# Rows of x for 12 of layer 0's 391 edge groups from one-hot products instead of gathers, in a two-layer graph network on one core

## The chip, the cores and the metric

The kernel runs on one core of a Trainium2 chip. The metric is the device time of one execution in microseconds (us). Three runs of the kernel before gave 4848.2 us as their median (4844.53 to 4863.56).

## The reference

There are 12,500 nodes with 48 features each and 200,000 edges, sorted by their destination. Cut to what matters:

```python
# layer 0
tmp = concat([x[dst], x[src], edge_attr_32], axis=1)      # 48 + 48 + 32 = 128 columns
msg = relu(tmp @ W1 + b1) @ W2 + b2
x1  = layernorm(x + segment_sum(msg, dst))
# layer 1
m   = relu(x1[src] + edge_attr_48)
out = layernorm(x1 + (1 + eps) * x1 + segment_sum(m, dst))
```

Because the edges are sorted by dst, a run of neighbouring edges touches only a short window of destination nodes. The sources are random, so x[src] and x1[src] need a row from anywhere in the table.

## The kernel before

The edges are cut into 391 groups of 512, each four tiles of 128 edges, one edge on each partition. The nodes are padded to 98 blocks of 128 rows; 14 segments of 7 blocks (896 rows) are finished one after the other.

**Rows of the sources.** GpSimd (POOL) issues one indirect DMA for each tile (`gather`, line 201), four a group, from x in layer 0 (`fetch0`, line 399) and from x1 in DRAM in layer 1 (`fetch1`). Each gather reads 128 rows of 192 bytes.

**Layer 0, group g.** The tile cat holds, for each edge, a one-hot of its destination in a window of 48 nodes, the gathered row, and the edge's 32 features. `fill0` (line 404) writes the features (ACT) and the one-hot (VectorE, line 302), and loads the window's rows of x @ W1a, computed beforehand by `project`, to the first 48 rows of the weights wcat (SP's queue, line 412). `turn0` transposes cat on TensorE into pt (line 417) and VectorE copies it to cat_t (line 419). `hidden0` multiplies it by wcat into ph (line 424), and ACT applies the bias and the relu. `message0` multiplies by W2 into pm (line 432), and VectorE adds b2. `sum0` multiplies the one-hots by the messages into pa (line 323), and VectorE adds pa to the segment's sums at a register offset (line 318).

**Layer 1, group g.** VectorE adds the gathered rows and the edge features (line 495), ACT applies the relu (line 497), and TensorE sums over the destinations as before (line 323).

**Products instead of gathers in layer 1.** For 28 of the 391 groups, every 13th from 26, nothing is gathered. `finish0` splits each finished segment of x1 into three bf16 pieces, whose sum is x1, and keeps them in SBUF (xp: 98 blocks, 3 pieces, 48 columns). `split_src` splits each source index into its row within a block and its block. `place` makes, for two groups at a time, a one-hot of the row times the block's number plus one, and transposes it. For each block b, `select` (line 525) compares this with b + 1 on VectorE, which leaves a one-hot in bf16 for those edges whose source lies in block b, and `multiply` (line 530) multiplies it by the block's three pieces and accumulates in PSUM. After all 98 blocks the three pieces are added (line 570).

**Order.** The order of every engine's work is that of the program (`manual_schedule`); semaphores are set from the tiles used. `run` walks in steps k and calls the stages with an offset: in layer 0, in step k, POOL fetches group k + 5, fill0 works on k + 2, sum0 on k - 3, message0 on k - 2, hidden0 on k - 1 and turn0 on k. Then comes `lead0` (line 457), which loads and projects segments in due steps. In layer 1 `lead1` calls `next(work1)` in each step, so the products go on by one batch of four blocks (BPS) a step: 32 products for two groups of four tiles. A generator that has done its 25 batches closes its pair of groups in one more step. There are ten cat buffers, so POOL can run ahead of TensorE by several groups. `finish0` comes in the stage of sum0, for the segment whose last group that is.

Of the kernel before, what the change touches and what calls it, by code (L numbers as in the profile page):

```python
# [24 lines left out]
F32 = mybir.dt.float32  # L25
I32 = mybir.dt.int32
BF16 = mybir.dt.bfloat16
AF = mybir.ActivationFunctionType
ALU = mybir.AluOpType
AX = mybir.AxisListType  # L30

P = 128
Q = 128
N = 12500
E = 200000
D = 48
# [4 lines left out]
NT = -(-N // Q)  # L41
NPAD = NT * Q
TPC = 4
CHUNK = P * TPC
NCHUNK = -(-E // CHUNK)
EPAD = NCHUNK * CHUNK

W = 48
R = 80
NB = 7  # L50
NSEG = NT // NB
# [4 lines left out]
AHEAD = 5  # L56
NW = 4
EC = 5
FIRST = 26
EVERY = 13  # L60
NPE = 28
BATCH = 2
PIECES = 3
BPS = 4

PE_GROUPS = [FIRST + EVERY * i for i in range(NPE)]
assert PE_GROUPS[-1] < NCHUNK and NPE % BATCH == 0

assert NSEG * NB == NT
STEP = CHUNK * N // E  # L70
# [58 lines left out]
def windowed(ctx, tc, dram, flag, x, src, dst, e32, e48, w1, b1, w2, b2, eps, out):  # L129
    nc = tc.nc  # L130
    const = ctx.enter_context(tc.tile_pool(name="const", bufs=1))
    onehots = ctx.enter_context(tc.tile_pool(name="onehots", bufs=2 * BPS))
    cats = ctx.enter_context(tc.tile_pool(name="cats", bufs=AHEAD + 5))
    echunk = ctx.enter_context(tc.tile_pool(name="echunk", bufs=3))
    work = ctx.enter_context(tc.tile_pool(name="work", bufs=2))
    aggs = ctx.enter_context(tc.tile_pool(name="aggs", bufs=3))
    node = ctx.enter_context(tc.tile_pool(name="node", bufs=2))
# [104 lines left out]
        nc.vector.tensor_copy(flag, pf)  # L242


    part = const.tile([P, NPE, TPC], F32, name="part")
    block = const.tile([P, NPE, TPC], F32, name="block")

    def split_src():
        first = FIRST * TPC
        some = src_i[:, first : first + (NPE - 1) * EVERY * TPC].rearrange(  # L250
            "p (i c) -> p i c", c=EVERY * TPC
        )[:, :, 0:TPC]
        last = src_i[:, PE_GROUPS[-1] * TPC : (PE_GROUPS[-1] + 1) * TPC]
        bits = node.tile([P, NPE, TPC], I32, name="bits")
        for op, by, plus, to in (
            (ALU.bitwise_and, Q - 1, 0.0, part), (ALU.logical_shift_right, 7, 1.0, block)
        ):
            nc.vector.tensor_scalar(bits[:, : NPE - 1, :], some, by, None, op0=op)
            nc.vector.tensor_scalar(bits[:, NPE - 1, :], last, by, None, op0=op)
            nc.vector.tensor_scalar(to, bits, plus, None, op0=ALU.add)  # L260


    def project(s):
# [37 lines left out]
    def one_hot(o, g):  # L301
        nc.vector.tensor_tensor(
            o, iota_w[:, None, :].to_broadcast([P, TPC, W]),
            rel[:, g, :, None].to_broadcast([P, TPC, W]), op=ALU.is_equal,
        )
# [53 lines left out]
    def rows_of(table, s):  # L359
        return table[s * SN : (s + 1) * SN, :].rearrange("(t p) d -> p t d", p=Q)  # L360

    def finish0(s):
        pn = segment_sums(0, s)
        y = node.tile([Q, NB, D], F32, name="y")
        nc.vector.tensor_tensor(y, pn, x_seg.pop(s), op=ALU.add)
        x1 = node.tile([Q, NB, D], F32, name="x1")
        layer_norm(x1, y)
        nc.sync.dma_start(rows_of(x1_dram, s), x1)
        for i in range(PIECES):
            piece = xp[:, s * NB : (s + 1) * NB, i, :]  # L370
            nc.scalar.activation(piece, x1, AF.Copy)
            if i < PIECES - 1:
                rest = node.tile([Q, NB, D], F32, name="rest")
                nc.vector.tensor_tensor(rest, x1, piece, op=ALU.subtract)
                x1 = rest

    def finish1(s):
        pn = segment_sums(1, s)
# [9 lines left out]
    def last_group(s):  # L388

        return max(g for g in range(NCHUNK) if low(g) < (s + 1) * SN)  # L390
# [3 lines left out]
        finishes.setdefault(last_group(s), []).append(s)  # L394


    cat, ph, h, pm, hot = {}, {}, {}, {}, {}

    def fetch0(g):
        cat[g] = cats.tile([P, TPC, Q], F32, name="cat")  # L400
        for j in range(TPC):
            gather(cat[g][:, j, W : W + D], x, g, j)

    def fill0(g):
        e = load_edges("e32c", e32, DE, g)
        nc.scalar.activation(cat[g][:, :, W + D :], e, AF.Copy)
        one_hot(cat[g][:, :, :W], g)
        s = seg_of(g)
        at = nc.sync.value_load(
            off[0:1, g : g + 1], min_val=low(g) - seg_start(s), max_val=high(g) - seg_start(s)  # L410
        )
        nc.sync.dma_start(wcats[g % NW][0:W, :], a_dram[s][bass.ds(at, W), :])

    def turn0(g):
        pt = psum.tile([Q, TPC, P], F32, name="pt", bufs=2)
        for j in range(TPC):
            nc.tensor.transpose(pt[:, j, :], cat[g][:, j, :], ident[:P, :P])  # L417
        cat_t = work.tile([Q, TPC, P], F32, name="cat_t")
        nc.vector.tensor_copy(cat_t, pt)  # L419
        h[g] = cat_t  # L420
# [36 lines left out]
    def lead0(k):  # L457
        for s in range(1, NSEG):
            if k == first_group(s - 1) + 4:
                load_seg(x, s)  # L460
            if k == first_group(s - 1) + 8:
                project(s)
        if k == 14:
            check_windows()
        if k == 16:
            split_src()

    for g in range(AHEAD):
        fetch0(g)
    project(0)  # L470
# [4 lines left out]
    )  # L475


    made = {}

    def fetch1(g):  # L480
        if g in PE_GROUPS:
            return
        cat[g] = cats.tile([P, TPC, D], F32, name="xs")
        for j in range(TPC):
            gather(cat[g][:, j, :], x1_dram, g, j)
# [5 lines left out]

    def message1(g):
        m = work.tile([P, TPC, D], F32, name="m")
        xs = made.pop(g) if g in PE_GROUPS else cat.pop(g)
        nc.vector.tensor_tensor(m, xs, h[g], op=ALU.add)  # L495
        msg = work.tile([P, TPC, D], F32, name="msg1")
        nc.scalar.activation(msg, m, AF.Relu)  # L497
        h[g] = msg
# [2 lines left out]
        pa = reduce_tiles(hot.pop(g), h.pop(g))  # L501
        add_window(1, g, pa)


    tiles = BATCH * TPC
    PER = 512 // (PIECES * D)
    SUMS = ("ph", "pm", "pt")

    def place(first):

        which = psum.tile([Q, tiles, P], BF16, name="pt", bufs=2)
        for i in range(BATCH):
            which_e = work.tile([P, TPC, Q], BF16, name="which_e")
            for j in range(TPC):
                nc.vector.tensor_scalar(
                    which_e[:, j, :], iota_q, part[:, first + i, j : j + 1],
                    block[:, first + i, j : j + 1], op0=ALU.is_equal, op1=ALU.mult,
                )
            for j in range(TPC):
                nc.tensor.transpose(which[:, i * TPC + j, :], which_e[:, j, :], ident16)  # L520
        return which

    def select(which, b):
        o = onehots.tile([Q, tiles, P], BF16, name="o")
        nc.vector.tensor_scalar(o, which, float(b + 1), None, op0=ALU.is_equal)  # L525
        return o

    def multiply(ps, o, b):
        for k in range(tiles):
            nc.tensor.matmul(  # L530
                ps[k // PER][:, k % PER, :], o[:, k, :], xp[:, b, :, :],
                start=False, stop=False, skip_group_check=True,
            )

    def edge_of(ps, start):
        for t in ps:
            n = t.shape[1] * PIECES * D
            nc.tensor.matmul(
                t.rearrange("p k c d -> p (k c d)"), zeros[:, :P], zeros[:, :n],
                start=start, stop=not start,  # L540
            )

    zeros = const.tile([1, 512], BF16, name="zeros")
    nc.vector.memset(zeros, 0.0)

    def products():

        for first in range(0, NPE, BATCH):
            due = PE_GROUPS[first]
            which = place(first)  # L550
            ps = [
                psum.tile([P, min(PER, tiles - k * PER), PIECES, D], F32, name=name,
                          bufs=2 if name == "pt" else 1)
                for k, name in enumerate(SUMS)
            ]
            edge_of(ps, True)
            last = []
            for b in range(0, NT, BPS):
                now = [(b + i, select(which, b + i)) for i in range(min(BPS, NT - b))]
                for c, o in last:  # L560
                    multiply(ps, o, c)
                last = now
                yield due
            for c, o in last:
                multiply(ps, o, c)
            edge_of(ps, False)
            xs = work.tile([P, tiles, D], F32, name="made")
            for k, t in enumerate(ps):
                n = t.shape[1]
                nc.vector.tensor_reduce(  # L570
                    xs[:, k * PER : k * PER + n, :], t.rearrange("p k c d -> p k d c"),
                    AX.X, ALU.add,
                )
            for i in range(BATCH):
                made[PE_GROUPS[first + i]] = xs[:, i * TPC : (i + 1) * TPC, :]
            yield due

    work1 = products()

    def lead1(k):  # L580
        next(work1, None)
# [216 lines left out]
```

## Time and profile before

| | us |
|---|---|
| median of the runs | 4848.2 (4844.53 to 4863.56) |
| the profiled execution's own time | 3846.41 |
| its span | 3844.6 |
| busy: POOL | 2887.0 (75%) |
| busy: TensorE (PE) | 2856.8 (74%) |
| busy: VectorE (DVE) | 1893.4 (49%) |
| busy: ACT | 564.0 (15%) |
| mean granted TensorE clock | 0.787 |

The profile is one execution, and it is 1002 us shorter than the median of the runs; its rows are durations in that execution. The page gives busy time by engine, then 40 equal slices of the span (the granted TensorE clock, PEclk, in tenths), then the costliest groups of instructions: line, engine, operation, tiles, count, busy time, mean ns of one, and the idle time of the engine just before them with what ended it ("issue" is idle time that ends for no reason that the profile shows). PEld is TensorE's weight load, which overlaps its products. Layer 0 lasts until about 1970 us, layer 1 from there to the end.

### The profile page before, as it was taken

The page shows a single profiled execution, that of the slowest core. Times are in us where ns is not written, and L with a number is a line of the kernel's source. Part 1 is how long each engine was busy: PE and PEld are TensorE (multiplying, and loading weights), DVE is VectorE, ACT ScalarE, POOL GpSimd, SP SyncE. Part 2 cuts the span into 40 slices and gives each one's busy share as a digit, 9 for nine tenths or more (in the row PEclk, how much of TensorE's full clock was granted, in tenths as well). Part 3 has the DMA queues.
Part 4 walks back from the last instruction along what each step waited for, and adds up shares of the span by engine and source line. Part 5 has one row for each costly group of instructions (what it writes and reads, how often), then busy time and mean ns, then how long its engine had stood idle before and what let it go on. Part 6 is the DMA issues. An engine that isn't in the chain of part 4 may idle for free. (4 is left out here: it accounts for less than half of the span.)

```text
span 3844.6 us, 67581 instructions
## 1 busy us (share of the span) xinstructions
PE 2856.8 (74%) x23396; PEld 2210.8 (58%) x23396; DVE 1893.4 (49%) x4618; ACT 564.0 (15%) x1329; POOL 2887.0 (75%) x3025
## 2 busy tenths in 40 slices
PE   6888788888888888888886767667677676667731
PEld 4555555556555555556565656656566666656631
DVE  3333333333333333333356766767677676767731
ACT  2222212212212212212110000000000000000000
POOL 7777777777777777777767777777777777777776
PEclk9787877787777777777778888878887887888765
DMA  3222222222222222222222221222122222212221
GB/s 71 43 45 49 44 44 47 46 40 49 49 39 49 45 41 47 48 41 46 38 44 39 50 39 37 55 45 43 38 50 43 45 43 50 43 33 55 45 42 28
DMA packets 293005, 171.68 MB, mean 45 GB/s; under 512 B 109664, under 2 KB 292400, under 8 KB 292656
## 3 DMA queue, kind: packets, MB, share of 16 engines
q0 software_dynamic: 96512, 74.31, 13.1%
q1 hardware_dynamic: 179248, 84.31, 8.0%
q10 hardware_dynamic: 16896, 8.69, 0.7%
q8 instruction: 185, 3.03, 0.3%
q14 instruction: 164, 1.34, 0.1%
HBM read 154.45 MB, written 12.62 MB: 43 GB/s over the span
## 5 line engine op out<-in xcount | busy, mean ns | idle before, releaser
L201 POOL DMA_INDIRECT cat<-in_x_dram,src_i x1564 | 1485.1, 950 | 481.0 <-issue 339.5
L201 POOL DMA_INDIRECT xs<-x_dram,src_i x1452 | 1400.0, 964 | 461.0 <-issue 340.7
L530 PEld LDWEIGHTS <-o 128*128 128x128 bf16 x10976 | 853.0, 112 | 22.6 <-DVE o L525 0.6
L525 DVE TENSOR_SCALAR o<-pt 128x1024 bf16<-128x1024 bf16 x1372 | 848.7, 677 | 5.4 <-PE pt L520 5.4
L419 DVE COPY cat_t<-pt 128x512 f32<-128x512 f32 x391 | 270.2, 691 | 897.5 <-PE pt L417 897.5
L323 PE MATMUL pa<-hot,msg 128*48 128x48 f32 x3128 | 255.8, 234 | 561.3 <-ACT msg L497 561.2
L417 PEld LDWEIGHTS pt<-ident,cat 128*128 128x128 f32 x1564 | 265.6, 176 | 632.2 <-DMA cat<-in_x_dram,src_i 365.1
L424 PE MATMUL ph<-cat_t,wcat 128*128 128x512 f32 x782 | 580.3, 833 | 0.8 <-DVE cat_t L419 0.8
L323 PEld LDWEIGHTS pa<-hot,msg 128*48 128x48 f32 x3128 | 202.6, 144 | 642.3 <-ACT msg L497 623.1
L530 PE MATMUL ph<-xp,o 128*128 128x144 bf16 x4116 | 568.5, 256 | 0.0
L417 PE MATMUL pt<-ident,cat 128*128 128x128 f32 x1564 | 389.4, 347 | 237.2 <-DMA cat<-in_x_dram,src_i 233.9
L530 PE MATMUL pm<-xp,o 128*128 128x144 bf16 x4116 | 563.9, 254 | 0.0
L432 PE MATMUL pm<-w_sb,h 128*128 128x48 f32 x3128 | 538.0, 326 | 1.3 <-ACT h L426 1.2
L432 PEld LDWEIGHTS pm<-w_sb,h 128*128 128x128 f32 x3128 | 484.0, 236 | 27.8 <-ACT h L426 2.4
L426 ACT ACTIVATE h<-ph,b_sb 128x512 f32<-128x512 f32 x391 | 268.4, 686 | 1370.1 <-PE ph L424 1355.6
L530 PE MATMUL pt<-xp,o 128*128 128x144 bf16 x2744 | 453.8, 253 | 0.0
L495 DVE TENSOR_TENSOR m<-xs,e48c 128x192 f32<-128x192 f32 x363 | 131.4, 362 | 549.6 <-DMA xs<-x_dram,src_i 549.0
L497 ACT ACTIVATE msg<-m 128x192 f32<-128x192 f32 x391 | 141.8, 363 | 1611.9 <-DVE m L495 1611.9
L323 PE MATMUL pa<-cat,msg 128*48 128x48 f32 x3128 | 260.8, 237 | 33.4 <-DVE msg L434 25.6
L323 PEld LDWEIGHTS pa<-cat,msg 128*48 128x48 f32 x3128 | 207.8, 147 | 112.1 <-issue 52.9
L434 DVE TENSOR_TENSOR msg<-pm,b_sb 128x192 f32<-128x192 f32 x391 | 139.5, 357 | 233.6 <-PE pm L432 231.3
L318 DVE TENSOR_TENSOR agg<-agg,pa 48x48 f32 x782 | 150.3, 192 | 174.0 <-PE pa L323 122.9
(79 smaller groups left out, 1066.8 us busy)
## 6 DMA issues: line engine op xcount, KB each, us to landing
e48c<-in_e_dram SPq DMA_DIRECT2D x78, 480.0 KB
cat<-in_x_dram,src_i POOLq DMA_INDIRECT x1564
e32c<-in_e_dram SPq DMA_DIRECT2D x78, 320.0 KB
xs<-x_dram,src_i POOLq DMA_INDIRECT x1452
wcat<-a SPq DMA_DIRECT2D x391, 24.0 KB
a<-a ACTq DMA_DIRECT2D x14, 256.0 KB
a<-a ACTq DMA_DIRECT2D x14, 192.0 KB
x_seg<-in_x_dram SPq DMA_DIRECT2D x14, 168.0 KB
```

The source lines that it names most:

```text
L201: nc.gpsimd.indirect_dma_start(out=t, out_offset=None, in_=table, in_offset=bass.IndirectOffsetOnAxis(ap=src_i[:, g * TPC + j : g * TPC + ...
L318: nc.vector.tensor_tensor(cols, cols, pa, op=ALU.add)
L323: nc.tensor.matmul(pa, msg[:, j, :], hot[:, j, :], start=j == 0, stop=j == TPC - 1)
L417: nc.tensor.transpose(pt[:, j, :], cat[g][:, j, :], ident[:P, :P])
L419: nc.vector.tensor_copy(cat_t, pt)
L424: nc.tensor.matmul(ph, wcats[g % NW], h[g], start=True, stop=True)
L426: nc.scalar.activation(t, ph, AF.Relu, bias=b1_sb)
L432: nc.tensor.matmul(pm[:, j, :], h[g][:, j, :], w2_sb, start=True, stop=True)
L434: nc.vector.tensor_tensor(msg, pm, b2_sb[:, None, :].to_broadcast([P, TPC, D]), op=ALU.add)
L497: nc.scalar.activation(msg, m, AF.Relu)
L525: nc.vector.tensor_scalar(o, which, float(b + 1), None, op0=ALU.is_equal)
L530: nc.tensor.matmul(ps[k // PER][:, k % PER, :], o[:, k, :], xp[:, b, :, :], start=False, stop=False, skip_group_check=True,)
```

## The change

In layer 0, 12 of the 391 groups (47, 73, ... 333, every 26th) are no longer gathered. Their rows of x come from one-hot products, one group at a time, by the functions that layer 1 uses. One batch of four blocks is done in each step from step 18: 16 products and four selects of half the width.

- xp holds the pieces of x during layer 0. They are made in steps 2 to 17: in each step one segment of x is loaded once more (`load_whole`, on SP's queue), and two steps later it is split.
- For the groups made so, `fetch0` only takes a cat buffer, and `fill0` copies the made rows into cat on ACT.
- xp is free for x1 from step 340. `finish0` splits x1 only for segments whose last group is 340 or later (12 and 13). The twelve before are loaded back from DRAM and split in steps 341 to 366, one every other step.
- PSUM: pt has one buffer instead of two; the selects read a tile of its own (which), and the sums have two banks of their own (sums0, sums1), with ph as the third in layer 1.
- `split_src` runs in steps 0 (layer 0) and 20 (layer 1) instead of 16.

```diff
-FIRST = 26
-EVERY = 13
-NPE = 28
-BATCH = 2
+BY_PRODUCT = ((47, 26, 12, 1), (26, 13, 28, 2))
+PE_GROUPS = [list(range(f, f + d * n, d)) for f, d, n, _ in BY_PRODUCT]
+SPLIT0 = 2
+BEGIN0 = 18
+END0 = 340
...
+    def split(t, s):
+        for i in range(PIECES):
+            piece = xp[:, s * NB : (s + 1) * NB, i, :]
+            nc.scalar.activation(piece, t, AF.Copy)
+            if i < PIECES - 1:
+                rest = node.tile([Q, NB, D], F32, name="rest")
+                nc.vector.tensor_tensor(rest, t, piece, op=ALU.subtract)
+                t = rest
+
+    whole = {}
+
+    def load_whole(table, s):
+        whole[s] = node.tile([Q, NB, D], F32, name="whole")
+        nc.sync.dma_start(whole[s], rows_of(table, s))
...
         nc.sync.dma_start(rows_of(x1_dram, s), x1)
-        for i in range(PIECES):
-            piece = xp[:, s * NB : (s + 1) * NB, i, :]
-            nc.scalar.activation(piece, x1, AF.Copy)
-            if i < PIECES - 1:
-                rest = node.tile([Q, NB, D], F32, name="rest")
-                nc.vector.tensor_tensor(rest, x1, piece, op=ALU.subtract)
-                x1 = rest
+        if last_group(s) >= END0:
+            split(x1, s)
...
+    def products(layer, sums):
+
+        n = BY_PRODUCT[layer][3]
+        tiles = n * TPC
+        for first in range(0, len(PE_GROUPS[layer]), n):
+            which = place(layer, first, n)
...
     def fetch0(g):
         cat[g] = cats.tile([P, TPC, Q], F32, name="cat")
+        if g in PE_GROUPS[0]:
+            return
         for j in range(TPC):
             gather(cat[g][:, j, W : W + D], x, g, j)
 
     def fill0(g):
         e = load_edges("e32c", e32, DE, g)
         nc.scalar.activation(cat[g][:, :, W + D :], e, AF.Copy)
+        if g in PE_GROUPS[0]:
+            nc.scalar.activation(cat[g][:, :, W : W + D], made.pop((0, g)), AF.Copy)
         one_hot(cat[g][:, :, :W], g)
...
-        pt = psum.tile([Q, TPC, P], F32, name="pt", bufs=2)
+        pt = psum.tile([Q, TPC, P], F32, name="pt")
...
-        if k == 16:
-            split_src()
-
+        if k in (0, 20):
+            split_src(k // 20)
+        if k >= BEGIN0:
+            next(work0, None)
+        for s in range(NSEG):
+            if k == SPLIT0 + s:
+                load_whole(x, s)
+            if k == SPLIT0 + s + 2:
+                split(whole.pop(s), s)
+            if last_group(s) < END0:
+                if k == END0 + 2 * s + 1:
+                    load_whole(x1_dram, s)
+                if k == END0 + 2 * s + 4:
+                    split(whole.pop(s), s)
+
+    work0 = products(0, ("sums0", "sums1"))
...
-    work1 = products()
+    work1 = products(1, ("sums0", "sums1", "ph"))
```

## The prediction

> **What bounds the kernel now.** I read the page first, then the waits of each engine, then a table of stretches, then the timeline at three places. The page names two engines that look equally full:
>
> ```profile
> PE 2856.8 (74%) x23396; PEld 2210.8 (58%) x23396; DVE 1893.4 (49%) x4618; ACT 564.0 (15%) x1329; POOL 2887.0 (75%) x3025
> ...
> PEclk9787877787777777777778888878887887888765
> ...
> L201 POOL DMA_INDIRECT cat<-in_x_dram,src_i x1564 | 1485.1, 950 | 481.0 <-issue 339.5
> L201 POOL DMA_INDIRECT xs<-x_dram,src_i x1452 | 1400.0, 964 | 461.0 <-issue 340.7
> ```
>
> The shares don't decide it; the gaps do. POOL's waits list hardly anything but pieces of 0.3 us: each gather takes about 0.95 us and is followed by 0.30 us of issue, with no other releaser of any length. TensorE, on the other side, waits for gathered rows all through layer 0 (PE pt on the DMA of cat 233.9 us, its weight loads 365.1). So POOL's gather stream sets the time of both layers. The only real hole in it is the change of layers:
>
> ```profile
> 1967.77 0.94 POOL L201 DMA_INDIRECT cat<-in_x_dram,src_i  x1 [0.30 <-issue]
> 1987.56 1.00 POOL L201 DMA_INDIRECT xs<-x_dram,src_i  x1 [18.85 <-issue]
> ```
>
> Layer 0's 1564 gathers start between 7.19 and 1967.77: 1960.6/1563 = 1.254 us each. Layer 1's 1452 start between 1987.56 and 3828.77: 1841.2/1451 = 1.269 us each. Four gathers a group make a step of 5.02 us in layer 0. The head (7.2), the hole (18.9) and the tail after the last gather (about 15) are the rest of the span of 3844.6 us.
>
> How near is TensorE behind? In the table of stretches (columns: length, then busy us of PE, PEld, DVE, ACT and POOL, then granted clock, DMA share and GB/s) layer 0 and layer 1 look like this:
>
> ```profile
> 900.00:1200.00 300.00, 251.68 (x1406) 174.61 (x1407) 101.08 (x266) 64.26 (x143) 226.96 (x240) 0.78 0.23 47
> ...
> 2600.00:2900.00 300.00, 209.06 (x2505) 187.52 (x2502) 208.83 (x481) 24.77 (x68) 228.08 (x237) 0.82 0.22 44
> ```
>
> 84% busy in layer 0 looks like no room, but it contains transposes that trickle in one by one behind their gathers. The room is read where TensorE is late and works without waiting. After a segment's finish it is some 15 us late, and at full clock it catches up like this:
>
> ```profile
> 1191.46 1.09 PE L424 MATMUL ph<-cat_t,wcat 128*128 128x512 f32 x2
> 1192.39 0.60 PE L417 MATMUL pt<-ident,cat 128*128 128x128 f32 x4
> 1192.92 0.56 PE L323 MATMUL pa<-cat,msg 128*48 128x48 f32 x8
> 1193.41 1.09 PE L432 MATMUL pm<-w_sb,h 128*128 128x48 f32 x8
> 1194.34 1.09 PE L424 MATMUL ph<-cat_t,wcat 128*128 128x512 f32 x2
> ```
>
> From ph to ph is 2.88 us: a whole group. At half clock (granted 0.50 in that stretch) the same takes 5.57 us:
>
> ```profile
> 1119.64 2.04 PE L424 MATMUL ph<-cat_t,wcat 128*128 128x512 f32 x2
> ...
> 1125.21 2.04 PE L424 MATMUL ph<-cat_t,wcat 128*128 128x512 f32 x2
> ```
>
> During both, POOL starts a gather every 1.25 us as before: the ten cat buffers let it run on while TensorE is up to some six groups late. The clock alternates: about 9 us at half, then full until TensorE has been sparse for some 10 us.
>
> **The change, part by part.**
>
> *Removed from POOL:* 12 groups x 4 gathers in layer 0, 48 x 1.254 = 60.2 us, all on the path.
>
> *Added to TensorE, in steps 18 to 329 of layer 0:* 98 blocks x 4 tiles x 12 groups = 4704 bf16 products, 16 a step. Their price is read from layer 1's batches of 32, at half and at full clock:
>
> ```profile
> 2804.04 3.44 PEld L530 LDWEIGHTS <-o 128*128 128x128 bf16 x32
> ...
> 2809.50 0.43 PEld L323 LDWEIGHTS pa<-hot,msg 128*48 128x48 f32 x8 [2.03 <-ACT msg L497]
> 2809.99 1.99 PEld L530 LDWEIGHTS <-o 128*128 128x128 bf16 x32
> ```
>
> 1.99/32 = 62 ns each at full clock, so 1.0 us a step; at half clock they stand 0.96 us per 8 apart (1989.8 to 1995), 1.92 us a step. Per group come 4 bf16 transposes and 4 products with zeros (some 0.05 us a step when spread). A step becomes 2.88 + 1.05 = 3.93 us at full clock and 5.57 + 1.97 = 7.54 at half clock. POOL's pace after the change is 5.02 x 379/391 = 4.86 us a step. So TensorE keeps up at full clock, not at half.
>
> Over a segment of 28 steps POOL needs 136 us. TensorE needs at full clock 28 x 3.93 = 110, plus 6 for project (1178.57 to 1184.76) and about 4 of waiting in finish0: 120. Each us at half clock does only 3.93/7.54 = 0.52 us of that work, so 16 us of room allow 33 us at half clock, a mean granted clock of 0.88. It has 0.78 today. Here a rule speaks: the Trainium skill ("TensorE: Matmul & The Clock Gate", section "What's actually happening") says that an idle window of about 3.4 us drops the clock to half and a busy one brings it back. By the row of today's layer 0, 0.78, TensorE would become the bound (second rival); by the rule, a step with 1 us of idle time in place of 2.1 seldom has an idle window. The trace sides with the rule in one respect: while TensorE is late and dense (1050 to 1070) the granted clock stays 1.00, and it falls only after two or three sparse steps. Being late therefore restores the clock. I take TensorE as hidden, with little to spare, and nothing for it.
>
> *Added to VectorE:* 98 x 12 = 1176 selects of half of layer 1's width. Layer 1 has four in 2.47 us, 0.62 each; half the width lies between 0.31 and 0.40 with a fixed share; I take 0.34, so 400 us in all, 1.36 a step. VectorE has 1.69 us a step of work now (101.08 x 5.02/300), so 3.1 of 4.86: hidden. What it may cost is POOL. The Trainium skill ("SBUF — State Buffer", section "SBUF: two separate sides") warns that a two-port VectorE operation locks GpSimd out while it makes the descriptors of a gather. If POOL stood still for every select, that is +400 us. The row is layer 1: with 849 us of wider selects its gathers are only 1.269 - 1.254 = 0.015 us apart more, 21 us in all. 400/849 of 21 is 10 us. Bounds 0 and 21; I take 10.
>
> *Splits of x in steps 4 to 17:* 14 segments, each one load of 168 KB on SP's queue, 3 ACT copies of 0.48 and 2 VectorE subtractions of 0.51 us. ACT then has 1.08 (64.26 x 5.02/300) + 1.45 of 5 us. SP's wcat loads queue behind one transfer a step; they are issued three steps ahead of their use (wait of SP on PE: 1413 us), so about 15 us of cover; uncovered each would cost its transfer, some 2 us x 14. POOL is 5 groups ahead. Nothing.
>
> *Splits of x1:* for segments 0 to 11 (last group 338 and before) the five operations leave finish0, which shortens VectorE's stall there by 2 us; they come back with a load of 168 KB each in steps 341 to 366, one every other step, while SP has only wcat and edge loads to carry. Segments 12 and 13 split as before, so the hole of 18.85 us stays. Nothing; the shorter stall can't gain either, since it lies on TensorE's and VectorE's side.
>
> *Waits:* ACT's copy of made into cat waits for VectorE's sum of the pieces, issued two steps (10 us) earlier; behind it on ACT stand the relus of h, for which TensorE's pm waits. VectorE waits at each group's start and end for TensorE (1 to 3 us every 26 steps), and cat_t and msg are queued behind it; TensorE's lateness absorbs it. One pt buffer instead of two: pt(g+1) stands behind ph(g) in TensorE's queue, which has waited for the copy out of pt(g) already. Nothing, and no gain, since none of this is on POOL; up to 12 x 3 = 36 us if TensorE has no room left.
>
> *Sum:* -60 + 10 = -50 us against the profiled execution's 3846.4, so 3796, -1.3%. The runs' median of 4848.2 is 1002 us above the profiled time, and no view shows where that lies. If it lay outside the gathers, -50 would hold: 4798. If it lies on the 3016 gathers, which fill 98% of the span, each is 0.33 us dearer, and 48 save 76: with the same 10 it is 4782. In proportion it is 4848.2 x (1 - 50/3846.4) = 4785. I take that.
>
> **The rivals.**
> *Faster, as summed:* 4770 to 4822. Chance 0.70.
> *No change:* TensorE gets late for good in some segments and gives back what POOL gains, or the unshown 1002 us hide POOL's gain. The same segment sum balances at 5.02 x 28 = 140.5 us, a mean clock of about 0.85. 4824 to 4872, chance 0.14. For it speaks how near 120 is to 136; against it the clock that recovers under load.
> *Slower:* TensorE becomes layer 0's bound because the clock stays at today's 0.78 despite the added work. In a time T a segment does T x (1 - 0.96 x 0.22) = 0.79 T of full-clock work; 120/0.79 = 152 us, +11.5 on each of 11 segments: +127 us on the profile, about 4975 in the runs. It decides from a clock of 0.85 down. For it: 0.78 over all of layer 0, with its 84% busy TensorE. Against it: the catch-up at 2.88 us. Chance 0.16.
> *It doesn't do what it says:* the waits of fill0 hold ACT up and POOL fills all ten buffers; it would show as POOL waits on cat and end among the no-changes.
>
> **How the numbers follow.** A measurement of this kernel can tell 0.5%, 24 us, from no change. Faster 0.70, same 0.14, slower 0.16. The likeliest case gives 4785. From its far end (no cost on POOL and 76 us saved, 4772, and a little for the medians) the range goes up through the no-change case, to 4855; the slower case is left out.
>
> **What would show it.** Right: 1516 gathers of cat at 1.25 to 1.27 us with gaps of 0.30, a start of layer 1 some 50 us earlier, a granted clock of 0.85 or more between 100 and 1650 us, and the same hole at the change of layers. Wrong: POOL gaps on cat that wait for PE pa (all buffers full) and no TensorE wait on gathers (TensorE is the bound); gathers of over 1 us beside the selects (the lock); a longer hole (the late splits).

## The result and the profile after

The changed kernel takes 4861.95 us (median of 20 runs, 4837.18 to 4888.94), the kernel before 4846.66 us on the same chip (20 runs, 4831.98 to 4863.56): a ratio of 1.0028, interval [1.0012, 1.0044]. The change was forecast to gain 63 us and costs 14 (0.0028 of 4846.66).

On some chips the kernel before takes 4837 to 4913 us (medians) and on others 3855 to 3857 us, with every run of it on a chip within 0.7% of that chip's median. Its first profile (3846.41 us), from which the prediction was worked, shows the second kind, while the result was timed on the first. I call them a 4850 chip and a 3856 chip. Each chip was visited once, so what goes with the chip and what with the visit is not told apart.

The profile of the changed kernel was taken on a 4850 chip (its own time 4855.34 us, span 4853.6 us). The lines that answer to those shown of before:

```profile
PE 3441.5 (71%) x28196; PEld 2681.6 (55%) x28196; DVE 2305.3 (47%) x5900; ACT 585.3 (12%) x1383; POOL 2836.8 (58%) x2977
...
PEclk8787787878887877877677777777777777777765
...
L204 POOL DMA_INDIRECT cat<-in_x_dram,src_i x1516 | 1437.8, 948 | 1031.4 <-issue 942.4
L204 POOL DMA_INDIRECT xs<-x_dram,src_i x1452 | 1397.0, 962 | 957.9 <-DVE m L600 466.1
```

A gather still takes 0.95 us and there are 48 fewer. But the idle time ahead of them is 1989 us where the first profile of before had 942, and POOL's share fell from 75% to 58%. POOL is no longer what sets the time. Its waits (us in total, times, longest) say the same:

```profile
POOL cat L204 <- issue: 942.4, 1417, 15.3
POOL xs L204 <- DVE m L600: 466.1, 156, 11.5
POOL xs L204 <- issue: 439.0, 1257, 39.3
```

1417 pieces of 0.30 us would be 425 us, and here they sum to 942. The trace has 429 gaps of over 0.65 us between one gather's end and the next one's start, half of them over 2.5 us, about one every 11 us and 1207 us in all (in the first profile of before one, of 19 us, at the change of layers). Rows land about 2.1 us after their issue, and they lie ready: in the kernel before on such a chip (before_again below) 267 gathers are issued and 265 landed when the transposes of step 60 start, which need 244. So POOL waits because the ten buffers are full, and the consumer is late. TensorE's own waits in the changed kernel:

```profile
PE sums L438 <- issue: 360.8, 568, 3.2
PE pa L345 <- issue: 274.6, 288, 13.3
PE pa L345 <- ACT msg L602: 124.6, 73, 13.2
PE ph L438 <- issue: 94.0, 154, 2.5
```

"Issue" is waiting for nothing that the profile shows. How it looks in the timeline (start, length, then the idle time before it in brackets):

```profile
1015.82 1.29 PE L518 MATMUL ph<-cat_t,wcat 128*128 128x512 f32 x2
1017.85 0.27 PE L511 MATMUL pt<-ident,cat 128*128 128x128 f32 x1 [0.73 <-issue]
1018.56 0.27 PE L511 MATMUL pt<-ident,cat 128*128 128x128 f32 x1 [0.45 <-issue]
1019.29 0.47 PE L511 MATMUL pt<-ident,cat 128*128 128x128 f32 x1 [0.46 <-issue]
1019.99 0.37 PE L511 MATMUL pt<-ident,cat 128*128 128x128 f32 x1 [0.22 <-issue]
1020.69 0.30 PE L438 MATMUL sums<-xp,o 128*128 128x144 bf16 x1 [0.33 <-issue]
```

Five matmuls start one every 0.70 us; without pauses four such transposes take 0.60 us together. I call such a gap of 0.64 to 0.78 us between the starts of two of TensorE's instructions (products and weight loads) a pause, and four or more with less than 1.5 us from one to the next a burst: the changed kernel has 921 pauses, in both layers, over half of them in bursts of some 5 us; the first profile of before has 42 and no burst. Some 640 of the 921 stand at instructions that wait for no semaphore at all, so that no operand can have held these up.

A second kind of lateness shows when the end of one engine's work is held against the start of the engine that needs it and is free. VectorE's and ACT's work reaches TensorE within 0.5 us (all but 22 of 1564 times, those at most 1.2 us). TensorE's work reaches them late: of the 391 relus of h in layer 0, 176 start over 0.5 us after TensorE's products ended with ACT idle, by up to 19.4 us and 436 us together. I call that a late signal of TensorE. The ends of products are modelled by the profiler, but the same reading of the first profile of before gives not one relu later than 0.4 us.

### The profile page after: what moved, and what is told of

The parts are those of the page before. It is cut to its first block, busy times and chain, and to the rows that moved or that the text cites. A ratio compares the mean times of both kernels' runs of the same rounds, so it can differ in the third digit from the quotient of the medians.

```text
span 4853.6 us, 78715 instructions
## 1 busy us (share of the span) xinstructions
PE 3441.5 (71%) x28196; PEld 2681.6 (55%) x28196; DVE 2305.3 (47%) x5900; ACT 585.3 (12%) x1383; POOL 2836.8 (58%) x2977
## 4 chain that ended last, share of the span: by engine, by line
PE 23%; another core or an unknown queue 12%; issue 12%; DVE 10%; DVEq 1%; ACT 1%; DMA 0%; POOL 0%; ACTq 0%
PE sums L438 9%; DVE o L433 5%; PE pa L345 5%; PE ph L438 3%; PE ph L518 2%; PE pm L526 2%; DVE m L600 1%; PE pt L511 1%; DVE hot L324 1%; DVEq L336 1%; DVE agg L340 0%; PE which L428 0%; ACT msg L602 0%; PE px L359 0%
## 5 line engine op out<-in xcount | busy, mean ns | idle before, releaser
L204 POOL DMA_INDIRECT cat<-in_x_dram,src_i x1516 | 1437.8, 948 | 1031.4 <-issue 942.4
L438 PE MATMUL sums<-xp,o 128*128 128x144 bf16 x12936 | 1457.8, 264 | 371.8 <-issue 360.8
L438 PEld LDWEIGHTS <-o 128*128 128x128 bf16 x15680 | 1331.7, 117 | 644.8 <-issue 601.0
L433 DVE TENSOR_SCALAR o<-which 128x1024 bf16<-128x1024 bf16 (+1 forms) x2548 | 1262.9, 555 | 61.5 <-remote 44.4
L438 PE MATMUL ph<-xp,o 128*128 128x144 bf16 x2744 | 503.1, 268 | 95.5 <-issue 94.0
L345 PE MATMUL pa<-hot,msg 128*48 128x48 f32 x3128 | 317.3, 246 | 331.8 <-issue 203.5
L345 PEld LDWEIGHTS pa<-hot,msg 128*48 128x48 f32 x3128 | 237.6, 153 | 432.1 <-issue 266.4
L511 PE MATMUL pt<-ident,cat 128*128 128x128 f32 x1564 | 319.3, 328 | 64.1 <-issue 56.0
L518 PEld LDWEIGHTS ph<-cat_t,wcat 128*128 128x128 f32 x782 | 149.8, 233 | 104.3 <-DVE cat_t L513 53.3
L324 DVE TENSOR_TENSOR cat<-iota_w,rel 128x192 f32<-128x192 f32 x391 | 135.4, 347 | 0.0
```

Source lines behind the costliest of these rows:

```text
L204: nc.gpsimd.indirect_dma_start(out=t, out_offset=None, in_=table, in_offset=bass.IndirectOffsetOnAxis(ap=src_i[:, g * TPC + j : g * TPC + ...
L324: nc.vector.tensor_tensor(o, iota_w[:, None, :].to_broadcast([P, TPC, W]), rel[:, g, :, None].to_broadcast([P, TPC, W]), op=ALU.is_equal,)
L345: nc.tensor.matmul(pa, msg[:, j, :], hot[:, j, :], start=j == 0, stop=j == TPC - 1)
L438: nc.tensor.matmul(ps[k // PER][:, k % PER, :], o[:, k, :], xp[:, b, :, :], start=False, stop=False, skip_group_check=True,)
L518: nc.tensor.matmul(ph, wcats[g % NW], h[g], start=True, stop=True)
```

## The experiments

The theories that the expectations name: S, TensorE gets its instructions in such trickles and sets the pace of both layers; G, each gather is dearer by 0.33 us in the runs than in the profile (one of the readings beside my scaling); V, selects, splits and waits cost the gain; D, the DMA traffic beside the gathers brings the pauses on. The kernels ran on six chips, each beside the kernel before (whose median is given): K 4913.2, L 4837.0, M 3856.2, N 3855.3, O 3856.7, P 4850.3 us.

**The kernel before once more (before_again, chip K), and on chip M (before_beside).**

> The kernel before, unchanged, with a new profile. Theory S (starved TensorE: in the usual execution TensorE gets its instructions in trickles, with pauses of 0.7 us that no operand explains, and so sets the pace of both layers; the first profile of the kernel before caught an execution without them): a span near 4845, several hundred pauses of 0.64 to 0.78 us on TensorE (42 in the first profile, 921 in the changed kernel's), gathers still 0.95 us each, and POOL idle between them for its buffers. Theory G (each gather is 0.33 us dearer outside the first profile): a span near 4845 with gathers or their issue gaps of 1.58 us together, evenly. If the span is 3845 again, the profiler itself takes the pauses away.

4906.22 us. Its gathers and TensorE's waits:

```profile
L201 POOL DMA_INDIRECT cat<-in_x_dram,src_i x1564 | 1482.9, 948 | 997.2 <-issue 850.4
L201 POOL DMA_INDIRECT xs<-x_dram,src_i x1452 | 1397.4, 962 | 995.8 <-DVE m L495 526.7
```

```profile
PE pa L323 <- issue: 463.4, 361, 10.0
PE ph L424 <- DVE cat_t L419: 166.5, 92, 6.9
PE pa L323 <- DVE msg L434: 165.0, 53, 9.8
PE ph L530 <- issue: 158.2, 261, 3.2
PE pm L530 <- issue: 154.6, 217, 2.5
```

G falls: a gather takes 948 and 962 ns here, 950 and 964 in the first profile. The 1000 us are gaps between gathers. TensorE has 677 pauses, as S expects, but nearly all in layer 1, where the products are. Layer 0 has 30 of them and is as much longer: its last gather starts at 2481.8 us, in the first profile at 1967.8. There the lines are like these:

```profile
1016.31 1.09 PE L432 MATMUL pm<-w_sb,h 128*128 128x48 f32 x8
1017.24 1.09 PE L424 MATMUL ph<-cat_t,wcat 128*128 128x512 f32 x2
1018.17 0.60 PE L417 MATMUL pt<-ident,cat 128*128 128x128 f32 x4
1022.22 0.36 DVE L434 TENSOR_TENSOR msg<-pm,b_sb 128x192 f32<-128x192 f32 x1 [5.05 <-remote]
1022.26 0.69 ACT L426 ACTIVATE h<-ph,b_sb 128x512 f32<-128x512 f32 x1 [6.14 <-remote]
1022.63 0.87 PE L323 MATMUL pa<-cat,msg 128*48 128x48 f32 x8 [3.87 <-DVE msg L434]
```

The products pm end at 1017.40 and VectorE, idle, adds their bias at 1022.22; ph ends at 1018.33 and ACT starts its relu at 1022.26. TensorE then follows VectorE within 0.1 us. So on such a chip it is TensorE's signals that come late, and TensorE waits in turn for those whom it kept waiting: 139 relus over 0.5 us late, 499 us together, and no signal to TensorE in layer 0 by more than 0.1 us.

> The kernel before once more, for its trace on the chip of these runs: a usual execution, 4820 to 4920 us, with 600 to 700 pauses of 0.70 us on TensorE in layer 1 and some 430 stalls of GpSimd for full buffers; layer 0 6.2 to 6.4 us a step. If it is 3850 us, the state of the first profile is one that executions fall into by chance.

3851.3 us: the other outcome that was named, but not by chance, since all seven runs of the kernel before on that chip are within 3849.92 to 3858.36. 54 pauses, no burst, and the waits of the first profile:

```profile
PE pa L323 <- ACT msg L497: 579.8, 301, 5.5
PE pt L417 <- DMA cat<-in_x_dram,src_i: 232.4, 304, 2.0
PE pt L520 <- DVE which_e L515: 57.7, 15, 6.5
```

TensorE waits for rows, and not for issue; none of its signals is over 0.5 us late. It is the chip that differs, or the visit to it.

**The changed kernel once more, on chip L and on chip N (after_again, after_third).**

> The changed kernel again, on the chip of these runs: 1.003 of the kernel before, with a layer 0 as long as before's (its last gather of cat near 2470 us) in spite of 48 gathers fewer, and POOL stalls of some 2 us about every eight gathers.

Chip L: 4857.04 us, ratio 1.005 [1.0026, 1.0074], 911 pauses.

> The changed kernel unchanged, once more beside the kernel before. On a chip like that of the last runs (the kernel before at 3856 us, no pauses of TensorE), my working would be read on the ground it was made on: 48 gathers fewer, 60 us, less what the split of x costs at the start, so 3795 to 3835 us, a ratio of 0.985 to 0.995; if the selects and products cost more there than they give, 1.000 or above. On a chip where the kernel before takes 4840 to 4920 us: a ratio of 1.000 to 1.007, as measured twice.

Chip N: 3798.59 us against 3855.34, ratio 0.9853 [0.9837, 0.987], as expected for such a chip. There the change gains 57 us. Its page and TensorE's waits:

```profile
PE 2906.4 (77%) x28196; PEld 2371.0 (62%) x28196; DVE 2293.5 (60%) x5900; ACT 582.6 (15%) x1383; POOL 2854.4 (75%) x2977
...
PEclk8899998999999999987787788878878888888855
...
L204 POOL DMA_INDIRECT cat<-in_x_dram,src_i x1516 | 1445.4, 953 | 466.3 <-issue 315.4
L204 POOL DMA_INDIRECT xs<-x_dram,src_i x1452 | 1407.1, 969 | 460.3 <-issue 335.7
```

```profile
PE pa L345 <- ACT msg L602: 570.3, 296, 5.4
PE pt L511 <- DMA cat<-in_x_dram,src_i: 131.3, 158, 2.2
```

The wait for gathered rows has shrunk from 232 to 131 us but is still there: GpSimd is the bound, TensorE a near second. 31 pauses.

**Without the one-hot products of layer 1 (no_products, chip K; no_products_2, chip P).** All 391 groups of layer 1 are fetched.

```diff
+PE_GROUPS = []
...
-    work1 = products()
+    work1 = iter(())
```

> The kernel before with no products at all: all 391 groups of layer 1 are gathered, and TensorE loses 10976 products and their weight loads. Theory S: TensorE has half the instructions in layer 1 and POOL sets its pace: (3128 gathers x 1.254) + 45 = about 3970 if the pauses vanish in layer 0 too, about 4300 if only in layer 1. Theory G: 4847 + 112 x 1.58 = 5025.

Chip K: 4848.01 us, ratio 0.9867 [0.9822, 0.9912].

> The kernel before with all 391 groups of layer 1 fetched and no one-hot products; 0.9867 of the kernel before on a chip where that takes 4913 us. On a chip where the kernel before takes 3856 us and GpSimd issues without stalls: 28 x 4 gathers more at 1.27 us, so 142 us longer, 3985 to 4005 us, a ratio of 1.033 to 1.039. If products are worth no more there than on the other kind of chip: 3856 us or below, a ratio under 1.005. On a chip of the slow kind: 0.98 to 0.99 again.

Chip P: 4795.49 us, ratio 0.9902 [0.9873, 0.993]. Neither S (3970 or 4300 us) nor G (5025) had it. With 112 more gathers the kernel is 1.0 to 1.3% quicker on such chips: these products cost there more than the gathers that they replace. What they save on a 3856 chip (142 us, an estimate from GpSimd's stream) was not timed, since both runs lay on 4850 chips. The pauses are gone (42 and 35, no burst), yet layer 1's gathers are still 1.45 to 1.46 us apart, not 1.27. TensorE, which has almost nothing to do there, starts its sums within 0.1 us of ACT, but VectorE starts adding them over 0.5 us late in 240 of 391 groups on chip K, by up to 20.4 us and 1397 us together (220 and 1387 us on chip P, none on a 3856 chip). So the lateness on such a chip is more than the trickles of 0.70 us, and theory S in its first form, which put all of it on them, is too narrow.

**The change in layer 0 alone (layer0_only, chip K).** The changed kernel without the products of layer 1 (their groups gathered).

```diff
-        if g in PE_GROUPS[1]:
-            return
...
-    work1 = products(1, ("sums0", "sums1", "ph"))
+    work1 = iter(())
```

> The changed kernel with products in layer 0 alone; layer 1 gathers all 391 groups. Theory S: layer 1 as without products, layer 0 as in the changed kernel (about 2440 us to its end), so 2440 + 1564 x 1.254 + 35 = about 4440. Theory G: the changed kernel's 4862 + 112 x 1.58 = 5040.

4874.1 us, ratio 0.992 [0.9892, 0.9947]; neither S (4440) nor G (5040). 335 pauses, now in layer 0. Beside no_products on the same chip its median is 0.5% longer with 48 gathers less, though the intervals overlap, and in the traces the last transposes of layer 0 come 28 us later (2531.1 for 2502.9): there the products of layer 0, too, seem to cost more than the gathers that they replace.

**The selects without the multiplies (layer0_selects, chip K; selects_2, chip P).** In layer 0 only the multiplies of the last blocks of each group stay.

```diff
-                for c, o in last:
+                for c, o in last if layer else []:
                     multiply(ps, o, c)
```

> The changed kernel without its products in layer 0 but for the last two blocks of each group (4608 of 4704 left out, so the made rows are not x): selects, splits and the 48 saved gathers stay. Theory S: TensorE's load of layer 0 is that of before, so the layer takes what it takes there or less, and the time falls to between 4700 and 4847. If the selects, the splits or the waits around them cost the gain (theory V), it stays near 4862. If only the gathers counted, 4787.

Chip K: 4889.07 us, ratio 0.9951 [0.9929, 0.9973].

> The changed kernel with all selects of layer 0 but without its multiplies, save those of the last two blocks of each group (so the rows of those 12 groups are wrong); 0.9951 of the kernel before on a chip where that takes 4913 us. On a chip where the kernel before takes 3856 us: if TensorE's products hide beside GpSimd's stream, the same as the changed kernel there, 3790 to 3808 us, a ratio of 0.983 to 0.988; if they cost time, less: 3760 us or below, a ratio under 0.976. On a chip of the slow kind: 0.993 to 0.998 again.

Chip P: 4811.12 us, ratio 0.9939 [0.9912, 0.9967]. The changed kernel has 1.0028 and 1.005, so the multiplies in layer 0 cost 0.8 to 1.1%, 37 to 54 us, on such a chip (a difference of ratios from different chips). On one chip, K, the traces say the same: the last transposes of layer 0 come at 2479.5 us here and at 2531.1 in layer0_only, whose layer 0 has the multiplies. Both ratios fit what was expected by S. What is left of the change gains about 27 us there: at the last transposes of layer 0 the kernel with selects is 23 us (K) and 31 us (P) ahead of the one without products, whose layer 0 is that of before.

**Half of the gathers (half_before and half_after, chip L; half_again, chip O).** The output is that of other rows.

```diff
     def gather(t, table, g, j):
+        if j % 2:
+            nc.gpsimd.memset(t, 1.0)
+            return
```

> The kernel before with every second gather left out (POOL fills those rows with ones instead, so the sums are not the reference's). POOL then has about 2 x 1.25 + 2 x 0.2 = 2.9 us a step in place of 5.0. If POOL were the bound of usual executions too (as the prediction had it), the time falls to TensorE's pace, 391 x (2.9 to 4) + 391 x (2.6 to 3.4): about 2600. Theory S (TensorE's pauses set the pace): the steps stay near 6 us and the time stays above 4500.

> The changed kernel with every second gather left out in the same way. Beside half_before it shows what the change adds off POOL: 24 us of POOL less are saved. Theory S: 312 steps x 1.05 to 1.97 us more of TensorE, so 330 to 600 us slower than half_before if TensorE is the bound there; if within 50 us of half_before, TensorE's added work is hidden behind something that neither POOL nor TensorE's own work is.

Chip L: 2985.45 us from the kernel before (ratio 0.6155 [0.6128, 0.6182]) and 3120.56 us from the changed one (0.6456 [0.6422, 0.6491]). TensorE's pauses fall to 120 and 44, from 637 in edges_once below and 911 in after_again on the same chip, with its work unchanged, and its late signals with them: 84 and 13 relus, 75 and 15 us together. No number that was named came true: S had over 4500 us for the kernel before and the bound by GpSimd about 2600, and the 135 us that the change costs lie between the 50 of hidden work and the 330 of work that is all on the path.

> The kernel before with every second gather replaced by a fill with ones (the output is that of other rows), which took 2985 us on a chip where the kernel before takes 4837 us. On a chip where the kernel before takes 3856 us: 2950 to 2990 us, a ratio of 0.765 to 0.775, if half the gathers are too few to bring the pauses on and both kinds of chip then do the same work in the same time; below 2900 us if the slow kind of chip costs something there too.

Chip O: the kernel before with half of the gathers takes 2714.57 us, ratio 0.7043 [0.7031, 0.7054]. That is the second outcome named (below 2900 us): the slow kind of chip costs something here too, and the kinds do not become equal. 4850 chips are 10% longer here (2985 to 2715), against 26% with all gathers (4850 to 3856).

**Half of the gathers, with GpSimd kept busy (half_paced, paced_again, paced_third; chips M, N, O).** A second fill, which nobody reads, stands in for the time of the gather (the output is that of other rows).

```diff
+    filler = const.tile([P, 900], F32, name="filler")
...
         if j % 2:
             nc.gpsimd.memset(t, 1.0)
+            nc.gpsimd.memset(filler, 0.0)
             return
```

> The kernel before with every second gather of both layers replaced by a fill of its rows with ones, and a second fill of a 128x900 tile that nobody reads, so that GpSimd stays about as busy as with the gathers (some 1.25 us a place) while half of the rows and of the DMAs are gone (the output is that of other rows). If the pauses of 0.70 us on TensorE come with the number of gathers (their DMAs, their semaphores), they stay away as in the half without filler, and the time is that of GpSimd's own stream, 3800 to 3950 us. If they come with the pace, that is with a consumer that is held up by GpSimd, they come back, with over 400 of them and a time of 4500 us or more.

> Every second gather replaced by a fill with ones and a fill of a 128x900 tile, as before (the output is that of other rows); it took 3153 us, 0.819 of the kernel before, on a chip on which the kernel before takes 3856 us. On a chip where the kernel before takes 4840 to 4920 us: if TensorE's pauses come with the number of gathers, some 3150 to 3250 us again (ratio 0.65) and no pauses; if with the pace of GpSimd, over 3900 us (ratio above 0.80) with some 300 pauses or more. On a chip of the first kind it takes 3153 us again and tells nothing new.

> Every second gather replaced by a fill with ones and a fill of a 128x900 tile (the output is that of other rows): 3153 us twice on chips where the kernel before takes 3856 us. On a chip where it takes 4840 to 4920 us: 3150 to 3250 us (ratio 0.65) without pauses on TensorE if the pauses come with the number of gathers; over 3900 us (ratio above 0.80) with some 300 pauses or more if they come with GpSimd's pace. On a chip of the other kind it tells nothing new.

3152.98, 3152.76 and 3151.84 us; ratios 0.8185 [0.8172, 0.8199], 0.8178 [0.8164, 0.8192], 0.8174 [0.816, 0.8187]. All three came to lie on 3856 chips, so the question (number of gathers or GpSimd's pace) was never put to a 4850 chip and stays open. The first expectation's 3800 to 3950 us rested on places of 1.25 us without a gather; the filler takes 0.865 us, and a gather and such a place together take 2.06 us in layer 0, not 2.5.

**Half of the gathers and no products in layer 1 (half_light, chip M).** The output is that of other rows.

> The kernel before with every second gather replaced by a fill with ones, and without the one-hot products of layer 1 (all 391 groups of layer 1 fetched, the odd tiles with ones; the output is that of other rows). In the kernel without products the signals of TensorE came up to 12 us late in layer 1 although TensorE had almost nothing to do there. If the number of gathers does that, half of them ends it and layer 1 takes 391 x 2 x 1.27 us plus the fills, about 1050 to 1150 us, and the whole about 2650 to 2750 us with next to no signal later than 0.5 us. If it is something else in the light stage, layer 1 stays above 1300 us and the signals stay late.

2457.17 us, ratio 0.6376 [0.6365, 0.6386], 16 pauses; some 1040 us from layer 0's last transposes to the end, and no signal of TensorE over 0.5 us late. On a 3856 chip, where that holds for every kernel (but for single signals of 0.5 to 0.6 us), it decides nothing.

**One load of the edge features (edges_once, chip L).** The kernel before with only the first chunk of e32 and e48 loaded and used throughout (the sums are of other edges).

```diff
-        if g % EC == 0:
+        if g == 0:
...
-            chunk[name] = echunk.tile([P, EC, TPC * width], F32, name=name)
+            chunk[name] = const.tile([P, EC, TPC * width], F32, name=name)
```

> The kernel before, loading only the first chunk of edge features of each layer and using it for all groups (156 of 158 edge loads left out, 62 of 172 MB, so the result is not the reference's). If the pauses come from the traffic of DMA (theory D: memory or its records), the time falls towards 3850. Theory S with pauses that belong to TensorE alone: within 1% of the kernel before.

4845.05 us, ratio 1.0009 [0.9984, 1.0035], 637 pauses. D falls for the edge loads; the traffic of the gathers was never taken away without the gathers.

**The changed kernel without the split of x (no_split, chip M).** In layer 0 the products are of zeros.

```diff
-            if k == SPLIT0 + s:
-                load_whole(x, s)
-            if k == SPLIT0 + s + 2:
-                split(whole.pop(s), s)
...
+    nc.vector.memset(xp, 0.0)
```

> The changed kernel without the split of x in the first groups: the pieces are zero in layer 0 (so the rows of its 12 product groups are zeros), while the products, the selects, the late splits of x1 and layer 1 stay. Theory that the split in the first 16 groups costs some 23 us which nothing gives back: 4825 to 4840 us on a chip where the changed kernel takes 4857, a ratio to the kernel before of 0.997 to 1.001, and steps 1 to 18 of layer 0 back at 6.8 us from 8.2. Theory that what is saved at the start is waited for later all the same: ratio 1.002 to 1.007, as for the changed kernel.

3808.37 us, ratio 0.9878 [0.9861, 0.9894], no better than the whole change on chip N (0.9853 [0.9837, 0.987]); from the copy of cat_t in step 1 to that in step 18 a step takes 4.78 us, 4.80 with the split. The split costs nothing on a 3856 chip. On 4850 chips the same steps take 8.2 us in the changed kernel and 6.8 before, which makes the expectation's 23 us. But most of that is a matter of when step 1 starts (31 us and 45 us on chip L): the copy of step 18 starts at 169 us in the changed kernel and at 161 before on chip L, at 172 in layer0_only and at 168 before on chip K. The 4 to 8 us that are left show on the 3856 chips too (112 for 104), with the split and without it.

## Why the prediction was wrong

**The step that failed** is the last of the sum: "The runs' median of 4848.2 is 1002 us above the profiled time, and no view shows where that lies", and then carrying -50 us over "in proportion". The 1002 us were no flat surcharge and no dearer gathers. They are another bound. On a 4850 chip GpSimd has gaps of over 1000 us and waits for full buffers; the consumers set the pace, with TensorE's late signals in both layers and its late starts where the products are. There the first conclusion of the working, "POOL's gather stream sets the time of both layers", does not hold, so the edit takes work from an engine that waits (27 us gained after selects and all) and gives 37 to 54 us to one that is late: +10 to +27, where +14 [+6, +21] was measured (0.0028 of 4847) and +24 on chip L. That the sum meets the measurement is no second proof, since the 37 to 54 us were taken from the same ratios; the 27 us are a reading of their own, from the traces. The no-change rival had this in half a sentence ("the unshown 1002 us hide POOL's gain"), at 0.14. A profile whose own time is 1002 us from its runs should have moved far more of the chance there.

**On the ground it was worked on, the sum held.** On chip N, beside the kernel before on chip M:
- Gathers: layer 0's first to last start takes 1906.2 us for 1957.9, -51.7. By number 48 x 1.2527 = 60.1; the pitch grew from 1.2527 to 1.2582, 0.0055 x 1515 = 8.4 us back. The prediction had 60.2 and 10.
- The hole at the change of layers, from the start of one gather to that of the next, is 19.1 us (17.7 before), layer 1 1848.3 us (1851.0). The span goes from 3849.5 to 3796.3, -53, where -50 was summed. The prediction's unscaled time was 3796 and the profiled execution took 3798.04; so close a meeting is luck in part, since the two profiles of before are 5 us apart.
- TensorE's step: 3.87 us from ph to ph at full clock, predicted 3.93, in the timeline of chip N:

```profile
1002.86 1.09 PE L518 MATMUL ph<-cat_t,wcat 128*128 128x512 f32 x2
1003.78 0.60 PE L511 MATMUL pt<-ident,cat 128*128 128x128 f32 x4
1004.22 1.16 PE L438 MATMUL sums<-xp,o 128*128 128x144 bf16 x16
1005.31 0.56 PE L345 MATMUL pa<-cat,msg 128*48 128x48 f32 x8
1005.80 1.09 PE L526 MATMUL pm<-w_sb,h 128*128 128x48 f32 x8
1006.73 1.09 PE L518 MATMUL ph<-cat_t,wcat 128*128 128x512 f32 x2
```

- The clock: the room asked for 0.88, and the same stretch has 0.95 (0.78 before), so it rises under load as the catch-up had suggested. The rule that the prediction leans on does not give the time that this takes: in the first profile TensorE is busy in all of 1075 to 1085 us and the clock stays at half from 1073.8 to 1084.1. (Columns as before; chip N, then the changed kernel's first profile.)

```profile
900.00:1200.00 300.00, 274.90 (x2469) 215.61 (x2469) 185.19 (x537) 63.33 (x143) 227.45 (x239) 0.95 0.21 47
```

```profile
900.00:1200.00 300.00, 249.49 (x1842) 188.45 (x1841) 140.14 (x405) 49.24 (x110) 175.76 (x187) 0.81 0.16 37
```

On the 4850 chip the same 300 us hold a quarter fewer matmuls (1842 for 2469), and the clock gets to 0.81 only. The slower rival's mechanism (TensorE the bound at a clock of 0.78) is near to what such a chip does, but the clock is not what makes such a chip long: half_before reaches 0.895 on one and is still 10% longer than half_again.

**Other steps.** The splits at nothing: held on chip M. VectorE's selects beside the gathers: 8.4 us at most, held. The selects read their input from PSUM, so this says nothing of the lock for operations between two places in SBUF. The signs named for "right" are all there on chip N: layer 1 starts 50 us earlier and the granted clock from 100 to 1650 us is 0.93. Of those named for "wrong", the changed kernel's first profile has the "POOL gaps on cat", though they end on "issue" and not on PE pa, and the wait of TensorE's products for rows is nearly gone (about 10 us, 131 us on chip N).

**What stays open.** Why the chips differ. Three things go with a 4850 chip: TensorE's signals, and with the products its starts, are late with no releaser; SP's 393 register moves take over 0.45 us in 41 to 67 cases in every trace from a 4850 chip and at most 42 ns in any from a 3856 chip, so TensorE is not alone; and halving the gathers takes most of the difference away (26% to 10%). That points to the supply of instructions or of signals beside a stream of gathers, but this is argued, not shown, and the gathers' number and GpSimd's pace were not told apart. The traces of 4850 chips also hold only a third of the semaphore events (23,700 of 69,069 for the kernel before). So a releaser named there, such as DVE m for POOL, is less sure than on the others, and "issue" can stand for a signal that was not recorded; the ends and starts of the work itself, from which the late signals are read, do not hang on these events. The loss of events raises a rival that no run tests: that recording the execution is itself what slows TensorE on such a chip. A granted clock was recorded in every execution of these experiments, so none shows the time without recording. No version was found that wins on both: of the kernels that do the whole work the changed one is the best seen on a 3856 chip, and the one without any products (0.987 and 0.990) on a 4850 chip; the latter was not timed on a 3856 chip.

## What to carry to other kernels

Before an edit is costed, the profiled execution's time must be held against the runs': when a fifth of the time is in no view, the profile's bound is not known to be the runs' bound, and a gain must not be carried over in proportion but taken again from a profile that has the runs' time. Work moved from one engine to another gains only where the first is the bound; the same edit gave -1.5% where GpSimd issued without gaps and +0.3% where TensorE was late. An idle gap with the releaser "issue" is worth a look of its own: 0.30 us after each gather is the price of gathering, gaps of 2.5 us were full buffers here. And where a chain of engines is late, the end of each engine's work should be held against the start of the next one's, in both directions: here that told which engine's signals came late.

## What the runs showed that was not expected

Chips of one type differ by 26% on this kernel (3856 to 4850 us), by 10% with half of its gathers, while the same instructions take the same time on both (a gather of layer 0 948 ns in before_again and before_beside, a select of 128x512 412 and 414 ns in the two of the changed kernel). On 4850 chips TensorE's signals to ACT and VectorE come late, by up to 24.8 us, while theirs to TensorE are never over 1.9 us late. On a 3856 chip TensorE's granted clock went up with the products in its gaps, from 0.78 to 0.95 in the same stretch of layer 0, and paid for part of the added work. And with half of the gathers the change costs 135 us on chip L, where it costs 24 with all of them; why it is 135 was not taken apart.
